# Adding fetched rows and cutting the sum at zero in one VectorE operation

## The chip, the cores and the metric

The kernel runs on one core of a Trainium2 chip. The metric is the device time of one execution in microseconds (us). Five engines work side by side, each through its own queue of instructions: TensorE (PE; its weight loads are shown as PEld) multiplies matrices, VectorE (DVE) and ScalarE (ACT) work on elements, GpSimd (POOL) issues the gathers here, and SyncE (SP) issues most other transfers. An engine's queue is named with a q (DVEq).

## The reference

One layer of a graph network over N = 12500 nodes with 48 values each and E = 400000 edges sorted by destination. For every edge, a hidden vector of 128 values is made from the two nodes and the edge's own 32 values, cut at zero, and the products of all edges into a node are added to that node.

```python
h = jnp.maximum(_layernorm(x, axis=-1), 0.0)
# edge_index = (src, dst)
x_i = h[dst]
x_j = h[src]
tmp = jnp.concatenate([x_i, x_j, edge_attr], axis=1)
hid = jax.nn.relu(tmp @ W1 + b1)
msg = hid @ W2 + b2
out = x + jax.ops.segment_sum(msg, dst, num_segments=N_NODES)
```

## The kernel before

The first matrix splits by rows: each node's share as a destination (table A) and as a source (table B) is computed once, in a first stage of about 100 us, and stored in memory; table B is also kept turned, 128 hidden values by nodes, in the tile `bt`. The main stage, `windows`, goes over 391 chunks (`NCH`) of 1024 edges, 8 tiles of 128 edges each. Destinations of a chunk lie in a window of W = 80 nodes, as the edges are sorted.

For chunk c, the program makes:

- `lhs`, an equality test of destination numbers against the window (VectorE, L463), under which the edge values are loaded, and `rhs`, 80 rows of table A and the edge weights. TensorE multiplies them into `pre` (L481), which lacks only the share of the sources.
- the sources' share, in one of three ways by tile. Most tiles are gathered in rows of table B by GpSimd into `gb` (L452), 6 or 7 tiles in a chunk, 2631 in all. 458 tiles are put together column by column from `bt` into `gt` (L393, VectorE and ScalarE, one column of 128 values each time, its place from a register) and added to `pre` by TensorE through a transposing product (L491). 36 tiles come as single rows by SyncE into `gr`.
- the hidden vectors `hid`: VectorE adds `gb` to `pre` (L517, or `gr` for a tile of single rows, L515), and later cuts the sum at zero in place (L530). Tiles that were turned by TensorE are complete in `pre` and are cut at zero from there (L532). "Turned" tiles are always the last of a chunk, or the last of each half.
- `hot`, an equality test of edges against the window (VectorE, L469). TensorE multiplies `hid` by `hot` into `p_g` (L541), and counts edges in the same way (L546). VectorE adds `p_g` to the segment `seg` (L560), at a place held in a register. After 12 chunks (`GQ`) a segment is finished: VectorE clears and copies into the other one (L576, L578), TensorE multiplies the finished one by the second matrix (L586, L587), and VectorE adds that to `xseg` (L588).

The order on each engine is the order in which the code is written. In iteration c, chunk c is prepared, chunk c-1 gets `before`, `turned`, `gathered` and `hidden`, and chunk c-2 gets `fold` and `add`. Column copies stand in four parts on VectorE (`columns(c, 0)` to `columns(c, 3)`); ahead of each part a register load (`load`, L358) brings the places of its 16 to 20 columns.

GpSimd's gathers run ahead of VectorE by up to 7 chunks, as `gb` has 8 buffers. To spread them, `mark` notes VectorE instructions with a weight in us, and gather j of chunk c waits for the instruction at that share of the weights, one of the iteration that freed the buffer (`paced`).

Of the kernel before, what the change touches and what calls it, by code (L numbers as in the profile page):

```python
# [1 line left out]

# [9 lines left out]
ALU = mybir.AluOpType  # L12
# [12 lines left out]
NCH = (NT + T - 1) // T  # L25
# [4 lines left out]
GQ = 12  # L30
# [63 lines left out]
def turned_at(c):  # L94

    return ((), (T - 1,), (T // 2 - 1, T - 1))[len(TURNED.get(c, ()))]
# [17 lines left out]
def single_at(c):  # L114

    return (0,) if c in BYROWS else ()
# [162 lines left out]
def windows(nc, tc, gp, bt, ident, idx, x_t, tab_a, tab_b, dst, edge_t, w1, w2s, b2s, out_t):  # L279
# [3 lines left out]
    with ExitStack() as es:  # L283
# [20 lines left out]
        for _, _, n, at in PARTS:  # L304
            nc.vector.tensor_scalar(
                last[:, :, at : at + n], last[:, :, at : at + n], 4, BT0,
                op0=ALU.mult, op1=ALU.add,
# [9 lines left out]
        for a, b in ((place, SEG2), (NEXT, SEG)):  # L317
# [7 lines left out]
            op0=ALU.mult, op1=ALU.add,  # L325
# [4 lines left out]
        def after(ins, of, reason):  # L330
            tc.add_manual_dep(
                ins, of.name,
                mybir.DependencyInfo(
                    mybir.DependencyClass.Sync, mybir.DependencyReason.DATA
                ),
                reason=reason,
            )
# [9 lines left out]
        def group(c):  # L347

            return divmod(c + OFF, GQ)

        def begin(g):
            return max(0, g * GQ - OFF)

        def numbers(c, at, n, engine):

            got = []
            for k in range(0, n, MOST):
                got += nc.values_load_multi_w_load_instructions(  # L358
                    last[c % P : c % P + 1, c // P, at + k : at + min(k + MOST, n)],
                    engines=[engine], min_val=0, max_val=1 << 23,  # L360
                    skip_runtime_bounds_check_because="numbers of nodes, and what is made of them",
                )[1]
            return got
# [6 lines left out]
        def load(c, part):  # L370

            dve, first, n, at = PARTS[part]
            n = max(0, min(n, len(BYCOLS) * P - ((c - COLS) * PART + first))) if c >= COLS else 0
            engine = mybir.EngineType.DVE if dve else mybir.EngineType.Activation
            if part == 0 and 2 <= c < NCH + 2:
                base, *nodes = numbers(c, at - 1, n + 1, engine)
                st[c - 2]["base"] = base
            else:
                nodes = numbers(c, at, n, engine) if n else []
            regs[c, part] = nodes  # L380

        def columns(c, part):

            dve, first, _, _ = PARTS[part]
            copy = nc.vector.tensor_copy if dve else nc.scalar.copy
            for k, at in enumerate(regs.pop((c, part), [])):
                of, e = divmod((c - COLS) * PART + first + k, P)
                if of not in gts:
                    gts[of] = gtp.tile([HID, P], F32, name="gt")
                at = at.with_bounds(  # L390
                    min_val=BT0, max_val=BT0 + 4 * (N - 1), guaranteed_mod_val=0, out_of_modulus=4
                ) - BT0
                done = copy(gts[of][:, e : e + 1], bt8[:, bass.ds(at, 4)].bitcast(F32))  # L393
                if dve:
                    mark(done, 0.06)
# [4 lines left out]
        def mark(ins, us):  # L400
            marks.append((ins, us))
# [15 lines left out]
        def singles(c):  # L417

            n = max(0, min(SINGLE, len(BYROWS) * P - (c - COLS) * SINGLE)) if c >= COLS else 0
            for k, row in enumerate(numbers(c, SINGLE_AT, n, mybir.EngineType.SP) if n else ()):  # L420
                of, e = divmod((c - COLS) * SINGLE + k, P)
                if of not in grs:
                    grs[of] = grp.tile([P, HID], F32, name="gr")
                row = row.with_bounds(min_val=0, max_val=4 * HID * (N - 1))
                nc.sync.dma_start(
                    grs[of].bitcast(U8)[e : e + 1, :],
                    tabb8[bass.ds(row, 4 * HID)].rearrange("(o h) -> o h", o=1),
                )
# [69 lines left out]
        def apart(c, x, by_cols):  # L498

            n = st[c]["n"]  # L500
            if not turned_at(c):
                return None if by_cols else x[:, :n, :]
            if len(turned_at(c)) == 1:
                return x[:, n - 1 : n, :] if by_cols else x[:, : n - 1, :]
            x, last_of = x.rearrange("p (b t) h -> p b t h", b=2), T // 2 - 1
            return x[:, :, last_of, :] if by_cols else x[:, :, :last_of, :]

        def gathered(c):

            s = st[c]  # L510
            s["h"] = h = wp.tile([P, T, HID], F32, name="hid")
            to, of, rows = apart(c, h, False), apart(c, s["pre"], False), apart(c, s["gb"], False)
            for t in single_at(c):
                gr = grs.pop(BYROWS.index(c))
                nc.vector.tensor_add(to[:, t, :], of[:, t, :], gr)  # L515
                to, of, rows = (x[:, t + 1 :, :] for x in (to, of, rows))
            added = nc.vector.tensor_add(to, of, rows)  # L517
            after(added.ins, s["behind"], "the rows are there when the product is")
            for fetch in s["fetches"]:
                tc.declare_no_dep(  # L520
                    added.ins, fetch, reason="the product that is waited for waits for the rows"
                )
            mark(added, 1.0)
            spans[c], marks[:] = list(marks), []

        def hidden(c):

            s = st[c]
            of = apart(c, s["h"], False)
            mark(nc.vector.tensor_scalar(of, of, 0.0, None, op0=ALU.max), 0.55)  # L530
            if turned_at(c):
                nc.vector.tensor_scalar(  # L532
                    apart(c, s["h"], True), apart(c, s["pre"], True), 0.0, None, op0=ALU.max
                )

        def fold(c):
            s = st[c]
# [26 lines left out]
        def segment_load(g):  # L564

            first, = numbers(begin(g), SEG, 1, mybir.EngineType.SP)
            xs[g] = xp.tile([D, L], F32, name="xseg")
            n = L if begin(g + 1) < NCH else END_L
            nc.sync.dma_start(xs[g][:, :n], x_t[:, bass.ds(node(first), n)])

        def segment_next(g):

            old, new = segs[g % 2], segs[(g + 1) % 2]
            if g > 0:
                for k in range(2):
                    nc.vector.memset(new[:, k, W:], 0.0)  # L576
            of, = numbers(begin(g), NEXT, 1, mybir.EngineType.DVE)
            nc.vector.tensor_copy(  # L578
                new[:, :, :W], old[:, :, bass.ds(of.with_bounds(min_val=0, max_val=FAR), W)]
            )  # L580
# [13 lines left out]
        with tc.manual_schedule():  # L594
            for c in range(NCH + 2):
                if c < NCH:
                    prepare(c)
                    singles(c)
                if c >= NCH:
                    load(c, 0)  # L600
                    columns(c, 0)
                load(c, 1)
                columns(c, 1)
                if 0 <= c - 1 < NCH:
                    before(c - 1)
                if 0 <= c - 2 < NCH:
                    fold(c - 2)
                if 0 <= c - 1 < NCH:
                    turned(c - 1)

                g, k = group(c - 2)
                if k == GQ - 3 or c == NCH - 1:
                    segment_load(g)
                if g > 0 and k < L // BLK:
                    segment_sum(g - 1, k, BLK)
                if g > 0 and k == STORE:
                    segment_store(g - 1, L)
                if 0 <= c - 1 < NCH:
                    gathered(c - 1)
                load(c, 2)  # L620
                columns(c, 2)
                if 0 <= c - 1 < NCH:
                    hidden(c - 1)
                load(c, 3)
                if 0 <= c - 2 < NCH:
                    add(c - 2)
                    if k == GQ - 1:
                        segment_next(g)
                columns(c, 3)
                for part in range(DVE_PARTS, len(PARTS)):  # L630
                    load(c, part)
                    columns(c, part)
                if c == NCH + 1:
                    segment_sum(g, 0, END_L)
                    segment_store(g, END_L)

                if c < PIECES:
                    s = slice(c * PIECE, (c + 1) * PIECE)
                    nc.sync.dma_start(out_t[:, s], x_t[:, s])
# [338 lines left out]
```

## Time and profile before

| | us |
|---|---|
| median of 3 runs | 3519.23 (3518.92 to 3527.93) |
| the profiled execution, its time | 3517.03 |
| its span, first to last instruction | 3515.3 |
| VectorE busy | 3234.7 (92%) |
| ScalarE busy | 3123.3 (89%) |
| GpSimd busy | 2660.5 (76%) |
| TensorE busy | 2616.9 (74%) |

Rows of groups read: line, engine, operation, tiles written and read, shapes, count; then busy time and the mean of one in ns; then idle time of the engine just before them and what ended it. Rows of the timeline read: start, duration (both in us), engine, line, operation, tiles, count, and in brackets the idle time before. Rows of the chain that ended last: start, length, what.

### The profile page before, as it was taken

The numbers are of one execution on the slowest core, as the hardware profiler recorded it, in microseconds if no ns is written. First come the engines' busy times: TensorE is split into PE (matmuls) and PEld (weight loads), VectorE is DVE, ScalarE is ACT, GpSimd is POOL, SyncE is SP. The second block draws the span as 40 slices with busy tenths as digits, with TensorE's granted clock in tenths as the row PEclk, the third lists the DMA queues.
The fourth block names the chain that finished last, engine by engine and source line by source line (L and its number), as shares of the span: only waits on it lengthen the run. The fifth ranks groups of instructions, "written<-read, shape, count | busy, mean of one in ns | idle before, by whom it ended". The sixth has DMA issues, their size and how long they took to land.

```text
span 3515.3 us, 119801 instructions
## 1 busy us (share of the span) xinstructions
PE 2616.9 (74%) x17111; PEld 2351.3 (67%) x17111; DVE 3234.7 (92%) x30218; ACT 3123.3 (89%) x31115; POOL 2660.5 (76%) x2658
## 2 busy tenths in 40 slices
PE   8677777777777776777777777777777777777777
PEld 5567666666676666666666766666667666676666
DVE  6799999999999999999999999999999999999997
ACT  5899998999998899989999899899999999898893
POOL 5777777777777777777777777777777777777775
PEclk9777777778777778778877787777777778778777
DMA  5533333333333333333333333333333333333332
GB/s 198 169 98 99 95 94 95 93 93 104 96 96 93 93 95 98 97 95 94 96 94 94 100 96 94 95 93 94 103 96 95 93 93 96 97 100 97 92 94 68
DMA packets 197238, 349.02 MB, mean 99 GB/s; under 512 B 67762, under 2 KB 104516, under 8 KB 195156
## 3 DMA queue, kind: packets, MB, share of 16 engines
q0 software_dynamic: 84224, 172.62, 19.3%
q1 hardware_dynamic: 111952, 168.56, 16.1%
q14 instruction: 658, 5.39, 0.5%
q8 instruction: 144, 2.36, 0.3%
q10 hardware_dynamic: 260, 0.10, 0.0%
HBM read 321.55 MB, written 22.07 MB: 98 GB/s over the span
## 4 chain that ended last, share of the span: by engine, by line
DVE 75%; PE 10%; ACT 5%; issue 4%; DVEq 3%; ACTq 0%; DMA 0%; SPq 0%
DVE gt L393 40%; DVE hid L517 9%; DVE hot L469 7%; DVE lhs L463 6%; DVE hid L530 6%; ACT gt L393 5%; PE p_g L541 4%; DVEq L358 3%; DVE seg L560 2%; DVE hid L532 2%; PE p_f L586 2%; PE p_f L587 2%; DVE xseg L588 1%; PE pre L491 1%; DVE seg L576 1%
## 5 line engine op out<-in xcount | busy, mean ns | idle before, releaser
L393 ACT COPY gt<-bt 128x1 f32 x31040 | 3076.9, 187 | 298.9 <-PE pre L491 195.5
L452 POOL DMA_INDIRECT gb<-tab_b,srci x2631 | 2639.0, 1003 | 821.8 <-issue 373.3
L393 DVE COPY gt<-bt 128x1 f32 x27584 | 1813.3, 143 | 147.6 <-issue 98.3
L541 PE MATMUL p_g<-hot,hid 128*128 128x80 f32 x6250 | 1069.5, 342 | 839.5 <-DVE hid L530 838.5
L541 PEld LDWEIGHTS p_g<-hot,hid 128*128 128x128 f32 x6250 | 1001.1, 251 | 913.1 <-DVE hid L530 903.5
L481 PEld LDWEIGHTS pre<-rhs,lhs 112*128 112x128 f32 x6250 | 963.0, 243 | 92.1 <-issue 91.6
L481 PE MATMUL pre<-rhs,lhs 112*128 112x128 f32 x6250 | 989.7, 326 | 20.0 <-DMA lhs<-in_edge_t 17.4
L517 DVE TENSOR_TENSOR hid<-pre,gb 128x896 f32<-128x896 f32 (+2 forms) x391 | 408.0, 1044 | 0.0
L469 DVE TENSOR_TENSOR hot<-wnum,rel 128x640 f32<-128x640 f32 x391 | 318.2, 814 | 0.0
L463 DVE TENSOR_SCALAR lhs<-row,bw 80x1024 f32<-80x1024 int16 x391 | 289.7, 741 | 10.0 <-DMA row<-in_dst 10.0
L491 PE MATMUL pre<-ident,gt 128*128 128x128 f32 x916 | 271.3, 404 | 17.5 <-issue 12.1
L530 DVE TENSOR_SCALAR hid<-hid 128x896 f32<-128x896 f32 (+2 forms) x391 | 244.9, 626 | 0.1
L546 PE MATMUL p_g<-hot,ones 128*128 128x80 bf16 x3125 | 240.0, 238 | 0.0
L546 PEld LDWEIGHTS <-ones 128*128 128x128 bf16 x3125 | 239.9, 132 | 0.0
L491 PEld LDWEIGHTS pre<-ident,gt 128*128 128x128 f32 x916 | 193.1, 269 | 20.1 <-issue 14.3
L560 DVE TENSOR_TENSOR seg<-seg,p_g 128x160 f32 x391 | 122.4, 313 | 7.5 <-issue 3.5
L532 DVE TENSOR_SCALAR hid<-pre 128x128 f32<-128x128 f32 (+1 forms) x389 | 118.0, 303 | 0.0
L588 DVE TENSOR_TENSOR xseg<-xseg,p_f 48x512 f32<-48x512 f32 (+1 forms) x67 | 45.0, 672 | 63.9 <-PE p_f L587 63.8
L586 PE MATMUL p_f<-seg,w2s 128*48 128x512 f32 (+1 forms) x134 | 102.8, 861 | 0.4 <-DVE seg L560 0.4
L587 PE MATMUL p_f<-seg,b2s 1*48 1x512 f32 (+1 forms) x134 | 90.7, 763 | 0.0
L587 PEld LDWEIGHTS p_f<-seg,b2s 1*48 1x48 f32 x134 | 12.6, 137 | 84.3 <-issue 83.1
L576 DVE MEMSET seg<- 128x944 f32 x64 | 54.1, 845 | 9.3
(67 smaller groups left out, 289.4 us busy)
## 6 DMA issues: line engine op xcount, KB each, us to landing
gr<-tab_b SPq DMA_DIRECT2D x4608, 0.5 KB
row<-in_dst SPq DMA_DIRECT2D x390, 160.0 KB
lhs<-in_edge_t SPq DMA_DIRECT2D x390, 128.0 KB
gb<-tab_b,srci POOLq DMA_INDIRECT x2631
rhs<-tab_a SPq DMA_DIRECT2D x391, 40.0 KB
xseg<-in_x_t SPq DMA_DIRECT2D x33, 192.0 KB
out_x<-xseg SPq DMA_DIRECT2D x33, 192.0 KB
tab_b<-tab SPq DMA_DIRECT2D x3, 1280.0 KB
```

Source lines behind the costliest of these rows:

```text
L393: done = copy(gts[of][:, e : e + 1], bt8[:, bass.ds(at, 4)].bitcast(F32))
L452: fetch = nc.gpsimd.indirect_dma_start(out=gb[:, t, :], out_offset=None, in_=tab_b[:, :], in_offset=bass.IndirectOffsetOnAxis(ap=srci[:, c ...
L463: mark(nc.vector.tensor_scalar(lhs[:W, : n * P], row[:, : n * P], bw[:, c : c + 1], None, op0=ALU.is_equal,), 0.8)
L469: mark(nc.vector.tensor_tensor(hot[:, :n, :], wnum.unsqueeze(1).to_broadcast([P, n, W]), rel[:, c * T : c * T + n].unsqueeze(2).to_broadca ...
L481: s["behind"] = nc.tensor.matmul(pre[:, t, :], s["lhs"][:K, t * P : (t + 1) * P], s["rhs"][:K, :], start=True, stop=t not in turned_at(c), ...
L491: s["behind"] = nc.tensor.matmul(s["pre"][:, t, :], gts.pop(j), ident, start=False, stop=True).ins
L517: added = nc.vector.tensor_add(to, of, rows)
L530: mark(nc.vector.tensor_scalar(of, of, 0.0, None, op0=ALU.max), 0.55)
L532: nc.vector.tensor_scalar(apart(c, s["h"], True), apart(c, s["pre"], True), 0.0, None, op0=ALU.max)
L541: nc.tensor.matmul(p_g[:, 0, :], s["h"][:, t, :], s["hot"][:, t, :], start=t == 0, stop=t == n - 1)
L546: nc.tensor.matmul(p_g[:, 1, :], ones, high[:, t, 1::2], start=t == 0, stop=t == n - 1)
L560: mark(nc.vector.tensor_add(to, to, s["p_g"]), 0.25)
```

## The change

The sum and its cut at zero become one VectorE operation, `TENSOR_ADD_SAT`, which gives max(min(in0 + in1, s0), s1) with s0 infinite and s1 zero. The separate maximum in place is taken out; the one on turned tiles stays. Weights of the pacing follow. The add to the segment, and the clearing of the next one, change places with the fourth register load.

```diff
+        def sum_kept(to, a, b):
+            return nc.vector._custom_dve(
+                dve_ops.TENSOR_ADD_SAT, out=to, in0=a, in1=b, s0=float("inf"), s1=0.0
+            )
 ...
             for t in single_at(c):
                 gr = grs.pop(BYROWS.index(c))
-                nc.vector.tensor_add(to[:, t, :], of[:, t, :], gr)
+                sum_kept(to[:, t, :], of[:, t, :], gr)
                 to, of, rows = (x[:, t + 1 :, :] for x in (to, of, rows))
-            added = nc.vector.tensor_add(to, of, rows)
+            added = sum_kept(to, of, rows)
 ...
-            mark(added, 1.0)
+            mark(added, 1.1)
 ...
         def hidden(c):
             s = st[c]
-            of = apart(c, s["h"], False)
-            mark(nc.vector.tensor_scalar(of, of, 0.0, None, op0=ALU.max), 0.55)
             if turned_at(c):
-                nc.vector.tensor_scalar(
+                mark(nc.vector.tensor_scalar(
                     apart(c, s["h"], True), apart(c, s["pre"], True), 0.0, None, op0=ALU.max
-                )
+                ), 0.25)
 ...
                     hidden(c - 1)
-                load(c, 3)
                 if 0 <= c - 2 < NCH:
                     add(c - 2)
-                    if k == GQ - 1:
-                        segment_next(g)
+                load(c, 3)
+                if 0 <= c - 2 < NCH and k == GQ - 1:
+                    segment_next(g)
                 columns(c, 3)
```

On VectorE, one iteration from the adding of rows to the next equality test read so before; `hid` are the hidden vectors, `pre` the products, `gb` the fetched rows, TENSOR_LOAD the register loads, and a count such as x16 stands for that many copies of one column:

```order
L517 TENSOR_TENSOR hid<-pre,gb 128x896
L358 TENSOR_LOAD last
L393 COPY gt<-bt 128x1 x7
L393 COPY gt<-bt 128x1 [waits Activation_49]
L393 COPY gt<-bt 128x1 x8
L530 TENSOR_SCALAR hid<-hid 128x896 [waits DVE_49]
L532 TENSOR_SCALAR hid<-pre 128x128
L358 TENSOR_LOAD last
L560 TENSOR_TENSOR seg_664<-seg_664,p_g 128x2x80
L393 COPY gt<-bt 128x1 x16
L463 TENSOR_SCALAR lhs<-row,bw 80x1024 [waits DMAHW7_49]
```

And the same place of the changed kernel, where the new operation is printed as ISA:

```order
L512 ISA hid<-pre,gb 128x896
L359 TENSOR_LOAD last
L394 COPY gt<-bt 128x1 x7
L394 COPY gt<-bt 128x1 [waits Activation_49]
L394 COPY gt<-bt 128x1 x8
L538 TENSOR_SCALAR hid<-pre 128x128
L566 TENSOR_TENSOR seg_664<-seg_664,p_g 128x2x80 [waits DVE_49]
L359 TENSOR_LOAD last
L394 COPY gt<-bt 128x1 x16
L464 TENSOR_SCALAR lhs<-row,bw 80x1024 [waits DMAHW7_49]
```

The maximum over `hid` is gone, and the segment add stands ahead of the register load instead of behind it. GpSimd's gathers keep their number and order.

More of the change, by code (lines that the diff above doesn't have):

```diff
@@ L4 @@
 import concourse.tile as tile
+from concourse import dve_ops
 from concourse import mybir
```

## The prediction

> **What bounds the kernel now.** I read the page first: the busy shares, the groups and the chain that ended last.
>
> ```profile
> PE 2616.9 (74%) x17111; PEld 2351.3 (67%) x17111; DVE 3234.7 (92%) x30218; ACT 3123.3 (89%) x31115; POOL 2660.5 (76%) x2658
> ...
> DVE 75%; PE 10%; ACT 5%; issue 4%; DVEq 3%; ACTq 0%; DMA 0%; SPq 0%
> ...
> L393 ACT COPY gt<-bt 128x1 f32 x31040 | 3076.9, 187 | 298.9 <-PE pre L491 195.5 <-issue 64.4 <-DMA gb<-tab_b,srci 5.1
> L452 POOL DMA_INDIRECT gb<-tab_b,srci x2631 | 2639.0, 1003 | 821.8 <-issue 373.3
> ```
>
> The first line says that VectorE (DVE) bounds and that GpSimd (POOL) has a quarter of the span free. The last line says otherwise: 821.8 us of idle time over 2631 gathers is 0.31 us each, and the timeline shows why.
>
> ```profile
> 50.87 0.96 POOL L452 DMA_INDIRECT gb<-tab_b,srci  x1 [19.76 <-DMA tab_b<-tab]
> 52.13 0.94 POOL L452 DMA_INDIRECT gb<-tab_b,srci  x1 [0.30 <-issue]
> ...
> 59.62 0.94 POOL L452 DMA_INDIRECT gb<-tab_b,srci  x1 [0.30 <-issue]
> ...
> 115.85 1.21 DVE L517 TENSOR_TENSOR hid<-pre,gb 128x1024 f32<-128x1024 f32 x1
> ...
> 3491.01 0.94 POOL L452 DMA_INDIRECT gb<-tab_b,srci  x1 [0.30 <-DVE xseg L588]
> ...
> 3502.68 0.81 DVE L517 TENSOR_TENSOR hid<-pre,gb 128x640 f32<-128x640 f32 x1
> ```
>
> Even the first gathers, before any pacing, come every 1.25 us: 0.94 of work and a fixed 0.30 between. From 50.87 to 3491.95 there are 2631 in 3441.1 us, 1.308 each, and the fixed 0.30 never becomes a wait. GpSimd therefore runs flat out all the way and takes 3441.1 / 391 = 8.80 us a chunk. VectorE goes from its first add of rows at 115.85 to its last at 3502.68 in 390 steps of 8.684 us. GpSimd is the slower of the two and lives on a head start: chunk 0's rows were issued 55 us before their add (60.56 to 115.85), the last chunk's only 10.7 us before (3491.95 to 3502.68). VectorE bounds this kernel, but the head start is nearly spent when it ends. So a faster VectorE cannot pull the end far forward by itself; what counts is the 63 ns by which a gather is longer than it need be.
>
> ```profile
> L452 POOL DMA_INDIRECT gb<-tab_b,srci x2631: 940/945/1783, 50.9 to 3491.0; - x188
> ...
> 1511.02 0.94 POOL L452 DMA_INDIRECT gb<-tab_b,srci  x1 [0.30 <-DVE gt L393]
> 1511.41 1.07 DVE L517 TENSOR_TENSOR hid<-pre,gb 128x896 f32<-128x896 f32 x1
> 1512.27 0.94 POOL L452 DMA_INDIRECT gb<-tab_b,srci  x1 [0.30 <-issue]
> 1512.41 1.04 DVE L393 COPY gt<-bt 128x1 f32 x16
> 1513.38 0.60 DVE L530 TENSOR_SCALAR hid<-hid 128x896 f32<-128x896 f32 x1
> 1513.52 1.29 POOL L452 DMA_INDIRECT gb<-tab_b,srci  x1 [0.30 <-DVE gt L393]
> ```
>
> The least gather takes 940 ns, so 2639.0 - 2631 x 0.940 = 165.9 us are stretch. The two gathers beside the add (L517) and the column copies (L393) take 0.94; the one beside the separate maximum (L530) takes 1.29. I put each gather over 0.96 us down to the VectorE operation that ran beside it. The maximum of L530 has 248 of them with 61.5 us, the equality test of L463 has 383 with 85.1, the clearing and copying of a segment 22 with 11.2; the other 1978 have 8.1 us together, 4 ns each. Those that start after L530 has ended, beside L532 and L560, are not longer (4 ns in the mean of 134). First and last of L530's and of L463's:
>
> ```profile
> 117.59 1.16 POOL L452 DMA_INDIRECT gb<-tab_b,srci  x1 [0.30 <-issue]
> 117.94 0.68 DVE L530 TENSOR_SCALAR hid<-hid 128x1024 f32<-128x1024 f32 x1
> ...
> 3484.27 0.63 DVE L530 TENSOR_SCALAR hid<-hid 128x896 f32<-128x896 f32 x1
> 3484.74 0.97 POOL L452 DMA_INDIRECT gb<-tab_b,srci  x1 [0.30 <-issue]
> ...
> 105.80 1.42 POOL L452 DMA_INDIRECT gb<-tab_b,srci  x1 [0.30 <-issue]
> ...
> 3479.42 1.27 POOL L452 DMA_INDIRECT gb<-tab_b,srci  x1 [0.30 <-DVE gt L393]
> ```
>
> **The change, part by part.**
>
> ```profile
> L517 DVE TENSOR_TENSOR hid<-pre,gb 128x896 f32<-128x896 f32 (+2 forms) x391 | 408.0, 1044 | 0.0
> L530 DVE TENSOR_SCALAR hid<-hid 128x896 f32<-128x896 f32 (+2 forms) x391 | 244.9, 626 | 0.1
> L463 DVE TENSOR_SCALAR lhs<-row,bw 80x1024 f32<-80x1024 int16 x391 | 289.7, 741 | 10.0 <-DMA row<-in_dst 10.0
> ```
>
> Removed on VectorE: 391 x 0.626 = 244.9 us of L530, which brings its own pace to 8.684 - 0.626 = 8.06 us a chunk.
>
> Removed on GpSimd: the 61.5 us by which L530 stretched gathers. (8.80 x 391 - 61.5) / 391 = 8.64 us a chunk are left, 0.58 more than VectorE then needs. So GpSimd takes over as the bound once the head start of 55 us is used up, after some 45 / 0.58 = 80 of the 391 chunks, and VectorE's other 0.58 us a chunk turn into waiting for rows.
>
> [...]
>
> The fused operation itself stands in no row. It reads and writes what L517 does, so its near rows are L517 (1.044 us, no stretch) and, if it should go through the data twice, L517 and L530 one after the other (1.670). [...] Either end moves only VectorE's pace, and the 0.58 us of slack covers all but the last 0.05 us of the upper one. The 36 adds of one row tile (L515, before) become the same operation at the same size, as nothing else about them changes.
>
> Moved: the fourth register load goes from ahead of the segment add to behind it. Such a load is exposed when the work queued ahead of it is short:
>
> ```profile
> 3470.94 0.74 DVE L463 TENSOR_SCALAR lhs<-row,bw 80x1024 f32<-80x1024 int16 x1
> 3471.88 1.24 DVE L393 COPY gt<-bt 128x1 f32 x19 [0.20 <-issue]
> ...
> L358 DVEq TENSOR_LOAD <-last x1590: 305/1153/4289, 108.2 to 3503.5; - x199
> ...
> 1503.19 0.28 DVE L532 TENSOR_SCALAR hid<-pre 128x128 f32<-128x128 f32 x1
> 1503.39 0.31 DVE L560 TENSOR_TENSOR seg<-seg,p_g 128x160 f32 x1
> ```
>
> Behind one operation of 0.74 us, 0.20 us are left open. The moved load has the turned maximum (L532, 0.28) and the add (0.31) ahead of it, 0.59 together, and before that copies that the engine has queued. Bounds are 0 and 1.153 - 0.59 = 0.56 us a chunk; I take 0.2, nearest to the row. VectorE then stands at about 8.26, still under 8.64, as it does even at the upper bound (8.62); the head start then lasts 120 chunks or more. What covers this cost is the wait for rows; without that cover it would be 0.2 x 391 = 78 us. The seg add's own wait is for the add of the chunk before, 8 us old. The pacing weights (1.1 and 0.25 in place of 1.0 and 0.55) only choose which VectorE instruction a gather waits for; with GpSimd some 50 us behind that instruction by the end, it never waits there.
>
> TensorE and ScalarE: 2616.9 / 391 = 6.7 and (3076.9 + 64.4) / 391 = 8.03 us a chunk, both below 8.64. TensorE's wait for the maximum turns earlier by L530's time and then becomes a wait for rows.
>
> The ends of the span: the first gather is released by the table's store and stays at 50.87. After the last gather:
>
> ```profile
> 3491.01 2.52 DMA gb<-tab_b,srci
> ...
> 3493.67 0.77 PE pre L481 x2
> 3494.43 3.33 PE p_g L541 x16
> ...
> 3502.76 0.74 DVE hid L517
> ...
> 3503.53 0.50 DVE hid L530
> ...
> 3509.87 0.48 DVE xseg L588
> ```
>
> This chain already starts at the landing of the last rows, so it moves as a whole, 3515.3 - 3491.95 = 23.35 us, less the 0.50 of the last maximum.
>
> The sum: 50.87 + (3441.1 - 61.5) + 22.85 = 3453.3 us of span, 1.7 around it (3517.03 against 3515.3): 3455. The median shown is 2.2 above the profiled execution, so 3457 against 3519.
>
> **What stays open in size** is L463. Its stretch depends on where in a gather it starts: 0.12 us when it begins 0.2 into one, 0.48 when it begins just ahead of one.
>
> ```profile
> 3462.32 1.06 POOL L452 DMA_INDIRECT gb<-tab_b,srci  x1 [0.30 <-DVE gt L393]
> 3462.53 0.73 DVE L463 TENSOR_SCALAR lhs<-row,bw 80x1024 f32<-80x1024 int16 x1
> ...
> 105.65 0.75 DVE L463 TENSOR_SCALAR lhs<-row,bw 80x1024 f32<-80x1024 int16 x1 [9.09 <-DMA row<-in_dst]
> ```
>
> The mean is 85.1 / 391 = 0.218. Once VectorE waits for rows it keeps step with the gathers, and the place may settle: 391 x 0.12 = 47 us or 391 x 0.48 = 188 in place of 85, so -38 or +103. Chunks of six and of seven gathers alternate with one and two turned tiles, which spreads it; I keep the mean.
>
> **The rivals.**
>
> [...] Chance 0.05.
>
> A long operation: if it costs L517 and L530 together, VectorE stays at 8.684 plus the load's 0 to 0.2, which gives the old time to 78 us more; at twice L517 (2.09) the pace is 9.10 and the end 115.85 + 390 x 9.10 + 16 = 3681. For no change 0.04, for slower 0.02.
>
> L463 settles badly: at 0.37 us a chunk the gain is gone, at 0.48 it is 3560. Half of it or less, 3480 to 3508, I give 0.06; no gain or a loss 0.03, a third of that on the slower side beyond 0.3%.
>
> The whole 244.9 us arrive (3274): the page's busy shares speak for it, but 2631 x 1.245 + 50.9 + 22.9 + 3.9 (around the span, and to the median) = 3353 is a floor that no faster VectorE lifts. Chance under 0.01; an end between 3353 and 3415, with L463 quiet as well, 0.04.
>
> **How the numbers follow.** The forecast, 3415 to 3480, has 0.75; with the smaller gains the range 3415 to 3505 holds about 0.8. Faster by over 0.3% (10.6 us, about what a measurement of this kernel can tell from no change) is 0.75 + 0.06 + 0.04 and some of the rest, 0.86; within it 0.06; slower 0.08.
>
> **What would show it.** Right: gathers from 50.9 on with a mean near 980 ns, only those beside the equality test and the segment clearing longer; the lead of the last gather of a chunk over its add falling to some 3 to 6 us by chunk 150; VectorE near 85 to 88% busy and idle before the fused add; TensorE's longest wait on rows (in the trace before it is 2.5 us, once). Wrong: a fused operation over 1.6 us, gathers of over 1.0 beside it, or gathers with gaps of more than 0.30.

## The result, and the profile after

The change took the median from 3521.72 to 3463.26 us (5 runs each), a ratio of 0.9835 with a 95% interval of 0.9822 to 0.9848. Forecast were 3457 from 3519, with 3415 to 3480 the likely range. The profiled execution took 3459.18 us, its span 3457.5. These times are from one chip; on the five chips that the experiments below were given, the median of the kernel before is 4477 to 4488 us, and the kernels traced there show ScalarE and VectorE pausing as described below, so times are compared only with that kernel's time on the same chip.

The page of the changed kernel: busy shares, the chain that ended last, and the groups that answer to those shown of before.

```profile
PE 2650.1 (77%) x17111; PEld 2343.4 (68%) x17111; DVE 3058.1 (88%) x29827; ACT 3123.0 (90%) x31115; POOL 2602.6 (75%) x2658
...
DVE 63%; ACT 10%; PE 10%; issue 8%; DVEq 3%; DMA 2%; ACTq 1%; POOL 1%; POOLq 0%
...
L453 POOL DMA_INDIRECT gb<-tab_b,srci x2631 | 2581.1, 981 | 822.5 <-issue 447.4
L394 DVE COPY gt<-bt 128x1 f32 x27584 | 1819.5, 144 | 263.3 <-issue 211.7
...
L512 DVE CUSTOM_DVE_ANT_0 hid<-pre,gb 128x896 f32<-128x896 f32 (+2 forms) x322 | 343.0, 1065 | 7.7 <-PE pre L492 7.4
L464 DVE TENSOR_SCALAR lhs<-row,bw 80x1024 f32<-80x1024 int16 x391 | 295.0, 755 | 9.7 <-DMA row<-in_dst 9.7
...
L512 DVE CUSTOM_DVE_ANT_1 hid<-pre,gb 128x768 f32<-128x768 f32 x69 | 65.3, 947 | 0.0
```

GpSimd's gathers fell from 2639.0 to 2581.1 us, 57.9 less, and the span by 57.8. Their idle time is the same 822 us as before, 0.31 each: they still run without a break, and what they gain is that they are shorter. The gathers' line, read by source, and the waits of the changed kernel:

```profile
L453 POOL DMA_INDIRECT gb<-tab_b,srci x2631: 940/944/1919, 51.2 to 3433.4; - x188
...
PE pre L492 <- DMA gb<-tab_b,srci: 153.3, 61, 4.8
```

Before, the last gather started at 3491.0, now at 3433.4: 57.6 of the 57.8 us. And TensorE now waits for rows 61 times, 153 us, up to 4.8 us. Before, the one such wait of any length was for the last rows (and one of 0.2 us):

```profile
PE pre L481 <- DMA gb<-tab_b,srci: 2.5, 1, 2.5
```

The rows have become what is waited for. In the timeline, a place like that of the prediction's rows from 1511.02 on, where a long gather stood beside the separate maximum:

```profile
1294.11 0.94 POOL L453 DMA_INDIRECT gb<-tab_b,srci  x1 [0.30 <-DVE gt L394]
1294.73 0.95 DVE L512 CUSTOM_DVE_ANT_1 hid<-pre,gb 128x768 f32<-128x768 f32 x1
1295.36 0.94 POOL L453 DMA_INDIRECT gb<-tab_b,srci  x1 [0.30 <-issue]
1295.59 1.05 DVE L394 COPY gt<-bt 128x1 f32 x16
...
1296.61 0.94 POOL L453 DMA_INDIRECT gb<-tab_b,srci  x1 [0.30 <-issue]
...
1297.86 1.27 POOL L453 DMA_INDIRECT gb<-tab_b,srci  x1 [0.30 <-issue]
1298.27 0.74 DVE L464 TENSOR_SCALAR lhs<-row,bw 80x1024 f32<-80x1024 int16 x1
```

Gathers beside the fused operation take 0.94 us (451 run beside it for 0.3 us or more, and none of them is over 960 ns); the long one in these rows, of 1.27 us, is that beside the equality test.

### The profile page after: what moved, and what is told of

It reads as the page before. It is cut to its first block, busy times and chain, and to the rows that moved or that the text cites. A ratio compares the mean times of both kernels' runs of the same rounds, so it can differ in the third digit from the quotient of the medians.

```text
span 3457.5 us, 119133 instructions
## 1 busy us (share of the span) xinstructions
PE 2650.1 (77%) x17111; PEld 2343.4 (68%) x17111; DVE 3058.1 (88%) x29827; ACT 3123.0 (90%) x31115; POOL 2602.6 (75%) x2658
## 4 chain that ended last, share of the span: by engine, by line
DVE 63%; ACT 10%; PE 10%; issue 8%; DVEq 3%; DMA 2%; ACTq 1%; POOL 1%; POOLq 0%
DVE gt L394 37%; ACT gt L394 10%; DVE hid L512 9%; DVE hot L470 6%; DVE lhs L464 6%; PE p_g L547 3%; DVEq L359 3%; DMA gb<-tab_b,srci 2%; DVE seg L566 2%; DVE hid L538 2%; PE p_f L592 2%; PE p_f L593 2%; PE pre L482 1%; PE pre L492 1%; DVE xseg L594 1%
## 5 line engine op out<-in xcount | busy, mean ns | idle before, releaser
L453 POOL DMA_INDIRECT gb<-tab_b,srci x2631 | 2581.1, 981 | 822.5 <-issue 447.4
L394 DVE COPY gt<-bt 128x1 f32 x27584 | 1819.5, 144 | 263.3 <-issue 211.7
L547 PE MATMUL p_g<-hot,hid 128*128 128x80 f32 x6250 | 1012.7, 327 | 436.8 <-DVE hid L512 408.8
L547 PEld LDWEIGHTS p_g<-hot,hid 128*128 128x128 f32 x6250 | 947.6, 238 | 505.9 <-DVE hid L512 460.0
L482 PEld LDWEIGHTS pre<-rhs,lhs 112*128 112x128 f32 x6250 | 1011.0, 254 | 160.0 <-issue 108.2
L482 PE MATMUL pre<-rhs,lhs 112*128 112x128 f32 x6250 | 1057.4, 340 | 61.7 <-PE pre L492 31.9
L512 DVE CUSTOM_DVE_ANT_0 hid<-pre,gb 128x896 f32<-128x896 f32 (+2 forms) x322 | 343.0, 1065 | 7.7 <-PE pre L492 7.4
L552 PE MATMUL p_g<-hot,ones 128*128 128x80 bf16 x3125 | 226.4, 229 | 0.0
L552 PEld LDWEIGHTS <-ones 128*128 128x128 bf16 x3125 | 223.5, 125 | 0.0
L512 DVE CUSTOM_DVE_ANT_1 hid<-pre,gb 128x768 f32<-128x768 f32 x69 | 65.3, 947 | 0.0
```

The costliest lines, as they stand in the source:

```text
L453: fetch = nc.gpsimd.indirect_dma_start(out=gb[:, t, :], out_offset=None, in_=tab_b[:, :], in_offset=bass.IndirectOffsetOnAxis(ap=srci[:, c ...
L482: s["behind"] = nc.tensor.matmul(pre[:, t, :], s["lhs"][:K, t * P : (t + 1) * P], s["rhs"][:K, :], start=True, stop=t not in turned_at(c), ...
L512: return nc.vector._custom_dve(dve_ops.TENSOR_ADD_SAT, out=to, in0=a, in1=b, s0=float("inf"), s1=0.0)
L547: nc.tensor.matmul(p_g[:, 0, :], s["h"][:, t, :], s["hot"][:, t, :], start=t == 0, stop=t == n - 1)
L552: nc.tensor.matmul(p_g[:, 1, :], ones, high[:, t, 1::2], start=t == 0, stop=t == n - 1)
```

## The experiments

Theory 1 is that of the prediction: gathers set the end, and the gain is the stretch that the separate maximum put on them. Theory 2, the rival, has VectorE's own time set the end in both kernels. None of the chips that the experiments were given is like that of the result, so the times that both theories name for such a chip could not be tested; what the traces show there of the gathers could.

### The parts of the change, one more copy, fewer gathers

The order alone, in the kernel before:

```diff
-                load(c, 3)
                 if 0 <= c - 2 < NCH:
                     add(c - 2)
-                    if k == GQ - 1:
-                        segment_next(g)
+                load(c, 3)
+                if 0 <= c - 2 < NCH and k == GQ - 1:
+                    segment_next(g)
```

> The kernel before, with the fourth register load behind the segment add and nothing else changed. Theory 1 (after the change, the gathers of GpSimd set the end; the gain is the stretch that the separate maximum put on them): the maximum is still there, its 248 long gathers with some 61 us too, and VectorE has 0.8 us of work ahead of the load, so nothing moves: 3515 to 3525 us. Theory 2 (VectorE sets the end in both kernels and the gain is its own time): if part of the gain is from the order, this kernel shows that part, 10 us or more; if none, 3520 too.

Measured: 4473.36 us against 4480.46, ratio 0.9978 (0.9960 to 0.9995). The order alone is worth next to nothing there, which both theories allow. The stretch beside the maximum stayed: 187 gathers with 54.8 us.

The fused operation with the old order (the same lines the other way round, in the changed kernel):

> The changed kernel with the fourth register load back ahead of the segment add. The load then has only the turned maximum (0.28 us) ahead of it, and the 0.21 us that it leaves open should become 0.3 to 0.4 a chunk, so VectorE alone would end 40 to 60 us later. Theory 1: VectorE alone would end at 115.9 + 390 x 8.43 + 14 = 3418 in the changed kernel, so 40 to 60 more is covered by the wait for rows, all or nearly all: 3460 to 3475 us. Theory 2: 3503 to 3523.

Measured: 4581.5 us, ratio 1.0224 (1.0205 to 1.0244). Neither theory has the fused kernel slower than before. No gather beside the fused operation was over 960 ns. The load in its old place left 0.39 us a chunk open ahead of the segment add, 154 us in all, as was expected; with the maximum no longer there, that is what the change of order avoids in part.

One more copy of one column a chunk, from PSUM into a spare tile, ahead of the fused add. At the 1819.5 / 27584 = 0.066 us of busy time that the page of the changed kernel has for a copy, 391 of them are 26 us of VectorE:

```diff
+        spare = one.tile([P, T, HID], F32, name="spare_of")
+        nc.vector.memset(spare, 0.0)
 ...
+                    nc.vector.tensor_copy(spare[:, 0, :1], wnum[:, :1])
                     gathered(c - 1)
```

> [...] Theory 1: VectorE has 45 us to spare over the run, so 3460 to 3467 us, no change to the changed kernel's 3463. Theory 2: 3463 + 26 = 3489.

Measured: 4551.92 us, ratio 1.0162 (1.0142 to 1.0182). The copies are busy for 58.0 us in their own row, 148 ns each, without regard to their overlap with others.

More single rows:

```diff
-SINGLE = 12
+SINGLE = 16
 ...
-WIDTH = 172
+WIDTH = 176
```

> The changed kernel with 16 in place of 12 single rows a chunk fetched by SyncE: 12 tiles fewer for GpSimd to gather (2619 in place of 2631), 12 more split adds on VectorE (about 0.15 us each, 2 us in all), 1.3 us a chunk more for SyncE, which is busy 69% of the time. Theory 1: 12 x 1.285 = 15 us less: 3446 to 3450 us. Theory 2: 3463 to 3466.

Measured: 4583.13 us, ratio 1.0233 (1.0214 to 1.0253). These four ran on one chip. The changed kernel itself did not run on that chip; on another of the five its ratio was 1.0191, as shown next, and against that the added copy costs nothing that shows and the 12 gathers taken away bring nothing. Neither says which theory holds on the chip of the result, since here the gathers no longer run back to back.

### The changed kernel again

> The changed kernel itself once more, on the chip that this comparison gets. The eight kernels so far ran on two chips on which the kernel before takes 4480 us in place of 3520, with ScalarE and VectorE idle for over 900 us each between column copies while they wait for nothing that the trace names, and on which four variants close to the changed kernel are 1.5 to 2.4% slower than before. Theory 1 (the gathers set the end where the copies are not held up): on a chip where the kernel before takes 3520, 3455 to 3470; on one where it takes 4480, GpSimd waits for VectorE in any case, so the stretch is worth nothing and the changed kernel takes 4540 to 4590. Theory 2 (VectorE's time sets the end everywhere): less VectorE work must be faster on every chip, so below 4400 where the kernel before takes 4480.

Measured: 4565.86 us against 4477.28, ratio 1.0191 (1.0166 to 1.0216), so the change loses there. Theory 2 falls as a rule for every chip: VectorE is busy for 3217.8 us there, against 3388.8 in the kernel with the order alone, and the kernel is slower. For the chip of the result this decides nothing. The range named for theory 1 was met, but it was read off the variants that had already run, so it does not speak for that theory. Groups and waits of that run:

```profile
L394 ACT COPY gt<-bt 128x1 f32 x31040 | 3257.4, 187 | 1140.4 <-issue 1087.8 <-remote 1.8 <-PE pre L492 0.8
L453 POOL DMA_INDIRECT gb<-tab_b,srci x2631 | 2623.2, 997 | 1845.3 <-DVE gt L394 569.1 <-issue 485.6 <-DVE hid L512 439.9
...
ACT gt L394 <- issue: 1087.8, 2370, 4.3
DVE gt L394 <- issue: 1044.2, 2249, 3.7
```

The second line is the answer to theory 1's condition: GpSimd is idle for 1845 us there, 1009 of them put down to the two VectorE groups in its row, where on the chip of the result it has 822 in steps of 0.3. A gather that is 57 us shorter in the sum ends nothing sooner when GpSimd waits. What differs most from the chip of the result are the pauses in the third and fourth lines, which are 65 and 212 us there. The timeline shows a train of them, a copy or two between pauses of half a us, on both engines at the same instants (four in five of VectorE's pauses between two copies end within 60 ns of one of ScalarE's):

```profile
2000.85 4.49 SPq L426 DMA_DIRECT2D gr<-tab_b  x9
2000.88 0.28 ACT L394 COPY gt<-bt 128x1 f32 x2 [0.55 <-issue]
2000.89 0.21 DVE L394 COPY gt<-bt 128x1 f32 x2 [0.27 <-issue]
...
2002.35 0.19 ACT L394 COPY gt<-bt 128x1 f32 x1 [0.53 <-issue]
2002.35 0.15 DVE L394 COPY gt<-bt 128x1 f32 x1 [0.57 <-issue]
...
2003.08 0.19 ACT L394 COPY gt<-bt 128x1 f32 x1 [0.54 <-issue]
2003.08 0.15 DVE L394 COPY gt<-bt 128x1 f32 x1 [0.58 <-issue]
```

### Without single rows

The trains often lie beside SyncE's single-row transfers, as in the first line above.

```diff
-BYROWS = single_tiles()
+BYROWS = []
```

> The changed kernel without single rows: the 36 tiles that SyncE fetched row by row (4608 transfers) are gathered by GpSimd like the others, 2667 gathers in place of 2631. Theory 1, where the kernel before takes 3520: 36 x 1.285 = 46 us more, 3505 to 3515. Theory 2, there: 36 split adds fewer, 3455 to 3463. Where the kernel before takes 4480 the pauses of ScalarE and VectorE come in trains of 0.73 us, half of those of 250 ns and more within 100 ns of a single-row transfer's start on SyncE; if these transfers make them, this kernel loses most of its 1088 and 1044 us of pauses and takes 3510 to 3800 there; if SyncE is only held along with the others, it stays within 2% of 4566.

Measured: 4493.75 us, ratio 1.0032 (1.0018 to 1.0045); the pauses are 1004 us on ScalarE and 968 on VectorE, 84 and 76 less than with the transfers, and the kernel is 72 us shorter than the changed one. So the transfers do not make most of the pauses. That SyncE is merely held along with the others is not shown. Without them the changed kernel is 1.6% nearer to the one before, and still does not beat it; the two ran on different chips.

### The missing maximum as mere load

```diff
+        spare = one.tile([P, T, HID], F32, name="spare_of")
+        nc.vector.memset(spare, 0.0)
 ...
             s = st[c]
+            of = spare[:, : T - 1, :]
+            nc.vector.tensor_scalar(of, of, 0.0, None, op0=ALU.max)
             if turned_at(c):
```

> The changed kernel with the old maximum put back at its old place and size (896 values in place), but over a spare tile whose values nobody reads: the fused add stays, VectorE's and GpSimd's load are as before the change. On a chip where the kernel before takes 3520: the 55 to 61 us of stretch return, 3510 to 3525 under both theories. On a chip where it takes 4480 and the changed kernel 1.9% more, two causes for that loss stand against each other. Theory A: the loss comes from the work that is missing (a long operation during which pauses in the issue of VectorE's next instructions cost nothing, or a gap that others use); with the maximum back as mere load the ratio is 0.995 to 1.005. Theory B: it comes from the fused operation itself or from the order; then the extra work does not help and the ratio stays at 1.015 or more.

Measured: 4544.37 us against 4478.67, ratio 1.0154 (1.0130 to 1.0178). By the expectation's own bounds that is theory B, if narrowly: the loss on those chips does not come, or not in the main, from the missing work. The order alone costs nothing (0.9978), and with the old order the loss is there as well (1.0224). So it comes with the fused operation or with what changed beside it, the weights of the pacing: gathers do wait for VectorE there (391.3 us for the fused operation in this kernel's trace), and no kernel parts the two. The operation's duration is not the reason (1066 ns for the group there, 1065 on the chip of the result).

What this kernel also shows is the stretch, brought back by a maximum over values that nobody reads:

```profile
2006.33 0.76 DVE L541 TENSOR_SCALAR spare_of<-spare_of 128x896 f32<-128x896 f32 x1
...
2015.70 1.15 POOL L456 DMA_INDIRECT gb<-tab_b,srci  x1 [1.06 <-DVE gt L397]
2016.12 0.62 DVE L541 TENSOR_SCALAR spare_of<-spare_of 128x896 f32<-128x896 f32 x1
2017.15 0.94 POOL L456 DMA_INDIRECT gb<-tab_b,srci  x1 [0.31 <-issue]
```

The maximum over the spare tile stands beside 245 gathers of over 960 ns, 67.4 us in all. The changed kernel, which has the same fused operation and no such maximum, has no long gather there. It is the form of the operation that stretches gathers, not what depends on it.

### Which operations stretch gathers

Five kernels vary that form. First an extra operation of 160 values from PSUM (0.314 us; the plain one), then one of 320 values from SBUF to SBUF, which takes twice the values in about the same time (0.365 us), both where the maximum stood. For a chip like that of the result theory 1 had 3460 to 3470 us with the first, its gathers no longer than before:

```diff
 ...
+            nc.vector.tensor_scalar(
+                spare[:, :2, :W], wnum.unsqueeze(1).to_broadcast([P, 2, W]), 0.0, None, op0=ALU.max
+            )
```

> The changed kernel with one more VectorE operation a chunk where the separate maximum stood: a maximum over 160 values from PSUM into a spare tile, about 0.31 us, of which the load behind the segment add hides some 0.2. [...] Theory 2: 3463 + 20 to 40 = 3483 to 3503.

```diff
 ...
+            nc.vector.tensor_scalar(
+                spare[:, :4, :W], spare[:, 4:, :W], 0.0, None, op0=ALU.max
+            )
```

> [...] Theory 1: at the old maximum's rate (0.25 us of stretch per us) or the equality test's (0.30), 391 x 0.31 x 0.25 to 0.30 = 30 to 36 us more than the plain one: 3492 to 3505 us, the mean gather 993 ns or so. Theory 2: the same as the plain one to 5 us, since VectorE's time is the same.

Measured: 4558.79 (ratio 1.0156, 1.0129 to 1.0183) and 4556.79 (1.0147, 1.0130 to 1.0164), the same in time. In the traces the one from PSUM stretched no gather and the other 59, by 6.5 us. That is 0.046 us of stretch for a us of the operation (142.9 us busy), where the expectation took the old maximum's 0.25; this short operation stretches less than in proportion. The 0.31 us for it in the expectation's sum was an estimate, which no run shows; 0.365 was measured.

Then the equality test for `lhs`, as a two-source operation with a zero that is in SBUF (the plain test):

```diff
+        zero = one.tile([P, 1], F32, name="zero")
+        nc.vector.memset(zero, 0.0)
 ...
-            mark(nc.vector.tensor_scalar(
-                lhs[:W, : n * P], row[:, : n * P], bw[:, c : c + 1], None, op0=ALU.is_equal,
-            ), 0.8)
+            mark(nc.vector.scalar_tensor_tensor(
+                lhs[:W, : n * P], row[:, : n * P], bw[:, c : c + 1],
+                zero[:W, :].to_broadcast([W, n * P]), op0=ALU.is_equal, op1=ALU.add,
+            ), 1.2)
```

> [...] Theory 1: GpSimd alone would end at 3374, VectorE alone at 3418 + 74 = 3492: VectorE is the bound again, 3480 to 3500 us, with a mean gather of some 948 ns and the head start of the gathers never used up. Theory 2: 3463 + 74 = 3537.

Measured: 4593.61 us, ratio 1.0224 (1.0206 to 1.0241). Theory 1's mean gather of 948 ns has the test's 87 us of stretch gone, and that was wrong, in direction too: the mean is 1022 ns, and the test now stands beside 266 long gathers with 196.9 us, where the one-source test of the changed kernel on another such chip has 300 with 121.8. The 74 us of VectorE's time in both sums were the author's estimate, and no run shows them; measured is the test itself, 1.271 us where the one-source test took 0.755 on the chip of the result. With fewer columns on VectorE and more single rows beside it:

> A version meant to beat both: the plain equality test, 66 in place of 71 columns a chunk copied by VectorE, and 16 in place of 12 single rows. VectorE: 3492 - 5 x 0.0655 x 391 (128) + 2 = 3366. GpSimd: 12 tiles fewer by single rows, 13 more for the columns left out: 3374 + 1 = 3375. Theory 1: the later of the two, 3370 to 3395 us. Theory 2: 3537 - 128 = 3409 or a little more.

Measured: 4665.78 us, ratio 1.0406 (1.0379 to 1.0432). The test stands beside 226 long gathers with 165.5 us. And the same with the zero in PSUM, in a column behind `wnum`:

```diff
-        wnum = ps_w.tile([P, W], F32, name="wnum")
+        wz = ps_w.tile([P, W + 1], F32, name="wnum")
+        wnum, zero = wz[:, :W], wz[:, W:]
 ...
+        nc.vector.memset(zero, 0.0)
```

> The equality test for lhs as a two-source operation whose second input, a zero, lies in PSUM in place of SBUF, with 66 columns a chunk on VectorE in place of 71 and 16 single rows in place of 12. With the zero in SBUF that test stretched gathers by 197 us (266 of them), against 87 to 113 for the one-source test; the add and the other equality test, each with one input in PSUM, stretch nothing. Theory 1: no gather beside this test is over 960 ns, on any chip; where the kernel before takes 3520 GpSimd ends at 3375 and VectorE at 3366, so 3370 to 3395. Theory 2: the stretch is no matter; 3409 there. Where the kernel before takes 4480: no gain expected, 4550 to 4670.

Measured: 4690.09 us, ratio 1.0465 (1.0444 to 1.0486), slower than every other variant, and worse than the 4670 allowed. Its gathers came out as expected: 307 of them run beside the test for 0.3 us or more, and none of these is over 960 ns. The timeline of the first kernel with the zero in SBUF, then of that with the zero in PSUM, and the latter's group:

```profile
2009.54 1.27 DVE L467 SCALAR_TENSOR_TENSOR lhs<-row,bw,zero 80x1024 f32<-80x1024 int16 x1
2009.77 1.86 POOL L456 DMA_INDIRECT gb<-tab_b,srci  x1 [0.67 <-DVE gt L397]
```

```profile
2024.53 1.27 DVE L466 SCALAR_TENSOR_TENSOR lhs<-row,bw,wnum 80x1024 f32<-80x1024 int16 x1
2024.77 0.94 POOL L455 DMA_INDIRECT gb<-tab_b,srci  x1 [1.07 <-DVE gt L396]
```

```profile
L455 POOL DMA_INDIRECT gb<-tab_b,srci x2634 | 2483.5, 943 | 2095.7 <-DVE gt L396 560.8 <-DVE hid L515 519.0 <-issue 480.8
```

Beside an operation of the same length the gather takes 1.86 or 0.94 us, by where one input lies, and with the zero in PSUM the mean of all 2634 is 943 ns against a least of 940 in the two traces of the result. So in these traces gathers are stretched by the long VectorE operations whose inputs all lie in SBUF, be it one tile or two, and not by those with one input in PSUM, the fused one among them. The copies of one column, from SBUF to SBUF too, do not stretch them (0.94 us at 1295.36 above); the clearing and copying of a segment does (12.6 us in the changed kernel on the chip of the result), and its parts were not told apart. That fewer long gathers bring time is not shown on these chips: this kernel has the shortest gathers and is the slowest.

## Why the prediction was right, point by point

**The bound.** Gathers without a break and a head start that runs out: the prediction's first part. After the change GpSimd sets the end, for which its unbroken gathers, TensorE's 153 us of waits for rows and VectorE's steps speak: 8.43 us a chunk while it had rows in hand, 8.69 from chunk 240 to the last. This rests on the comparison of the two traces; no kernel varied the gathers on a chip like that of the result. VectorE had to become faster as well. At its old 8.684 us a chunk it would have ended near 3515 whatever the gathers did, so the gain is the smaller of two savings.

**The gain.** 61.5 us was forecast. The maximum's stretch is gone wholly, the equality test's rose from 85.1 to 87.3 us (337 gathers) and that of clearing and copying segments from 11.2 to 12.6, so 57.9 came. The open term, where the test falls in a gather, stayed at its mean: 0.223 us a chunk for 0.218.

**The ends.** First gather at 51.2 for 50.87; 23.1 us behind the last gather (3457.5 less 3433.4 and 0.94) for 22.85. The sum, 3453.3, missed the span by 4.2: 3.6 of it in the stretch.

**The fused operation** was counted in the forecast at the add's 1.044 us, an estimate from that row. It costs what the add did, 408.3 us for 408.0 with both of its names in the page, so the cut at zero took no time of its own that shows, and it holds up no gather: none of the 451 beside it is over 960 ns. The nearer row was the right one.

**The moved load** was taken at 0.2 us a chunk. It left 81.8 us open, 0.21 a chunk, and the load behind the equality test 111.8 where it was 82.8. (Only the segment add changed places with the load; the clearing of the next segment stood behind the load before, too.)

```profile
2136.16 1.06 DVE L394 COPY gt<-bt 128x1 f32 x16 [0.21 <-issue]
...
2138.15 1.24 DVE L394 COPY gt<-bt 128x1 f32 x19 [0.28 <-issue]
```

**VectorE's own pace was mis-sized,** which the result did not feel. 8.06, with the load 8.26, was forecast; while it had rows in hand it went at 8.43 (chunks 8 and 165, 157 steps), and at 8.69 when it had not (chunks 240 and 390, 150 steps):

```profile
183.36 1.08 DVE L512 CUSTOM_DVE_ANT_0 hid<-pre,gb 128x896 f32<-128x896 f32 x1
...
1506.99 1.08 DVE L512 CUSTOM_DVE_ANT_0 hid<-pre,gb 128x896 f32<-128x896 f32 x1
...
2141.45 0.95 DVE L512 CUSTOM_DVE_ANT_1 hid<-pre,gb 128x768 f32<-128x768 f32 x1
...
3445.12 0.81 DVE L512 CUSTOM_DVE_ANT_0 hid<-pre,gb 128x640 f32<-128x640 f32 x1
```

The step that failed is 391 x 0.626 = 244.9: durations of neighbours overlap. In the rows of the prediction the maximum of 1513.38 starts before the copies of 1512.41 have ended, and VectorE's busy time, which counts overlapping time once, fell by 176.6 us only (3234.7 to 3058.1). In the 157 steps from chunk 8 to 165 it fell by 0.455 us a chunk, and idle time rose by 0.207, as the load's 0.2 had it; that makes 8.68 into 8.43.

So the 0.58 us of slack a chunk, 0.38 with the load, was not there. At 8.43 VectorE alone would end at 115.9 + 390 x 8.43 + 12.4 = 3416, 41 us ahead of the end that GpSimd set, 0.1 a chunk. That this was still enough was in part luck. That the upper bound of the load (0.56) would still be covered was wrong too: it set one pace against the other and left out that the head start lets VectorE be the bound as long as it lasts. Even at the 8.62 named there, VectorE would end at 115.9 + 390 x 8.62 + 12.4 = 3490. The head start lasted past chunk 200, not 80 to 120, and the sign that the prediction named, a lead of 3 to 6 us by chunk 150, did not come: the lead of a chunk's last gather over its add was 22.8 us at chunk 140, 21.3 at 150 and 4.3 at 240.

**Rivals.** The chance of 0.05 was the author's estimate for a fused operation that stretches gathers as the separate maximum did; it stretches none, nor is it long (1065 ns in its first row on the page), and the equality test did not settle badly. The whole 244.9 us did not arrive, and were not there to arrive.

**What stays open.** What the pauses on the other chips are. Why the kernels with the fused operation take 1.5 to 2.2% more there, where neither its length nor the missing work explains it. They have more of the pauses: on one and the same chip, the kernel with the order alone has 955 us on ScalarE and 772 on VectorE, and the fused one with one copy more 1066 and 996. Their granted TensorE clock is lower too (0.628 in the changed one, 0.667 with the order alone, 0.784 for the changed one on the chip of the result). Either may be cause or effect. And whether more VectorE work is free, and a gather less worth 1.285 us, on a chip like that of the result: tried, but not on such a chip.

## What to carry to other kernels

An engine that shows 75% busy can be the bound: look at the gaps between its instructions, and at whether the work that it does ahead is used up in the course of the run. When work is taken off an engine, ask also what that work does to its neighbours. Here two engines were nearly level, and both had to become faster; the end moved by the neighbour's 58 us, the smaller saving, and not by the 245 that the removed operation took by itself. A slack that is fed by a head start is counted over the run, not by the chunk.

## What the runs showed of the hardware that was not expected

A two-source VectorE operation of 1.27 us with its inputs in SBUF lengthened gathers more than a one-source one of 0.75 on the same 1024 values: 266 gathers with 196.9 us (1.86 us for the one shown, where 0.94 is the least) against 300 with 121.8. With one input in PSUM it lengthened none: of the 307 beside it none is over 960 ns. What in a gather is held up, no run tells. And the same kernel took 3520 us on one chip and 4480 on five others, where the kernels traced show ScalarE and VectorE with some 770 to 1190 us of pauses each, most of VectorE's at the same instants as ScalarE's; a change worth 1.65% on the first cost 1.9% on one of the others.
